# Two layers of graph aggregation and expert blocks: one zero tile for two lists, registers and first tokens at other places, stores on another queue

## The chip, the cores and the metric

The kernel runs on one core of a Trainium2 chip. The metric is the time of one execution on the device in microseconds (us), less is better. Engines are named as in the profile: PE (matrix products and transposes), PEld (its weight loads), DVE (vector), ACT (scalar functions), POOL and SP (issues most DMAs). A trailing q (SPq, PEldq) is the engine's instruction sequencer.

## The reference

The input is x (3327 rows of 256) and a sparse adjacency matrix adj (3327 x 3327). Two layers follow, each an aggregation and a mixture of experts, all on layer-normalized rows and added to x:

```
x = x + relu(adj @ (norm(x) @ W) + b)                             # layer 0, graph
x = x + sum over the top 2 of 8 experts of p_e * FFN_e(norm(x))   # relu, hidden 1024
filt = tanh(adj * adj) * (adj > 0); keep the 700 largest of each row
x = x + relu(filt @ (tanh(norm(x) @ Wp + bp) @ Wg) + bg)          # layer 1, graph
x = x + norm(x) + sum over the top 2 of 8 experts of p_e * FFN_e(norm(x))  # gelu, hidden 256
```

The weights p_e are a softmax over the two largest of eight gate scores.

## The kernel before

Rows are padded to 26 tiles of 128. `x` and the features `s` stay on chip. The adjacency is read twice, as 13 panels of 256 columns, each in two chunks of 1664 KB. A chunk goes into one of the six places of `ring`, called ring_77 to ring_82 in the listings; SP issues the loads (L340), three panels ahead. A panel is 104 products on PE (L358), some 22.5 us.

After each panel `after0` (layer 0) or `after1` (layer 1) works on that panel's two tiles. DVE adds bias and relu (L322, L323), normalizes (L288), forms the gate scores with 16 products (L378), ranks them (L406 to L417), and forms `rt_both`, which expert takes which row. ACT takes the exponential for the softmax (`rt_d`, L443) and DVE finishes the weights (L445 to L447). One panel later `list_tokens` counts rows per expert on PE (`pr`, L464 and L465) and POOL scatters the rows with weight and number (columns WT and ID of a 258-wide row) into a DRAM list, `xlist0` or `xlist1`, in which expert e has NP rows from e*NP (L482).

In layer 0, ACT also counts the non-zeros of every chunk: eight `sign` activations per chunk (L1046, 0.64 us and 0.19 us for reading the sum). ACT works in the order of its queue, so an exponential stands behind the signs listed ahead of it.

The first 256 rows of every expert's part are filled beforehand with zero rows whose ID points to spare output rows. This is `fill`: for each expert it takes a buffer of the pool `blk` (two buffers), clears it on POOL, writes the IDs, and SP stores it (L1013). `fill(xlist0)` is written after panel 0 and `fill(xlist1)` after panel 1; with SP's order, five fills come before panel 3's first load, four behind it, four behind the next, three behind the one after. Ahead of all of them SP issues two transposing copies of the gates, DRAM to DRAM, element by element (L1062).

Once enough tokens are listed, expert blocks of 256 rows ("pairs") run on PE: layer 0 blocks 0 to 29, layer 1 blocks t = 0 to 31 (8 early ones, 18 late pairs, 6 singles of 128 rows). For each block SP loads two table entries into registers (L815, L785), then rows (`xlist`, L820), w1 (L827), b1 (L831), and in layer 0 and for the first blocks of layer 1 also w2 and b2 (L838, L842). PE transposes the rows into `ptb` (L853), DVE (layer 0) or ACT (layer 1) copies that to `xT` (L856), PE forms `ps_h` (L865), ACT applies bias and function (L872, `narrow` in layer 1), PE forms `ps_y` (L904), DVE adds b2 (L911) and scales by the weight (L912), and POOL scatters the result to `ys` (L482). `step` turns the tokens of block t+1 between the two products of block t; block 0's tokens are turned in its own step, after the last panel.

Layer 1 ends in a branch (`inner`, L1297). The usual arm calls `know` first, which loads the expert numbers of the last eight blocks into registers of PE and DVE (L789), and then steps through the late blocks. Between steps it loads finished output rows back (`load_outputs`, ys, L968), adds them to x (`add_loaded`, L982, two additions for each pair of tiles) and stores x to `out` (L1304, on SP). Such a step of pairs is counted by k: k = 0 to 6 are the first 14 tiles, k = 7 to 10 the next 8. The last four tiles come in `finish` after block 31 (L968, L982, and L1266 on ACT's queue).

Of the kernel before, what the change touches and what calls it, by code (L numbers as in the profile page):

```python
# [22 lines left out]
P = 128  # L23
# [67 lines left out]
def gnn_moe_two_layers(  # L91
# [142 lines left out]
    def plain(name, a):  # L234
        t = const.tile(list(a.shape), F32, name=name)
        nc.gpsimd.dma_start(out=t, in_=a)
        return t
# [12 lines left out]
        )  # L250

    g1_bp_sb = plain("g1_bp_sb", g1_bp)
    g1_wg_sb = by_feature("g1_wg_sb", g1_wg)


# [113 lines left out]
    def rows_of(a, t0, n):  # L369
        return a[t0 * P : (t0 + n) * P, :].rearrange("(n p) d -> p n d", p=P)  # L370
# [381 lines left out]
    def experts(xlist, ys, group, fixed, n_hidden, func, w1T, b1, w2T, b2, copy, kept=None):  # L752
# [2 lines left out]

        own_n, all_w2, all_b2 = kept or (EARLY + LATE, None, None)
        pool, several = blk, []
        hc_n = n_hidden // P  # L760

# [15 lines left out]
        def expert(t, late, engines):  # L777

            table, col = late[0] if t >= EARLY else early_table, col_of(t)
            if known and t >= EARLY:  # L780
                if col < known[0]:
                    return col % E
                if engines != [SP]:
                    return known[1][col - known[0]]
            return nc.values_load(table[0:1, 0, col : col + 1], engines=engines, min_val=0, max_val=E - 1)  # L785

        def know(n, late):

            _, registers = nc.values_load_multi_w_load_instructions(  # L789
                late[0][0:1, 0, n : LATE_PAIRS + fixed], engines=[PE, DVE], min_val=0, max_val=E - 1  # L790
            )
            known[:] = [n, registers]

        def col_of(t):
            return t if t < EARLY else order[t - EARLY]
# [9 lines left out]
        def load_one(late):  # L805
            t = len(loaded)
            table = late[0] if t >= EARLY else early_table
            col, n = col_of(t), groups_of(t)
            base = FREE_PAN * NCHUNK + t * places

            def view(name):
                q, at, n = where[name]
                return ring[(base + q) % RING][:, at : at + n]

            row = nc.values_load(  # L815
                table[0:1, 1, col : col + 1], engines=[SP], min_val=0, max_val=E * NP - n * P
            )
            e = expert(t, late, [SP])
            xb = view("xb")[:, 0 : n * RW].rearrange("p (g d) -> p g d", g=n)
            d = nc.sync.dma_start(  # L820
                out=xb, in_=xlist[ds(row, n * P), :].rearrange("(g p) d -> p g d", p=P)
            )
            follow(d, early_rows if t < EARLY else rows_written)
            if t < EARLY:
                tc.add_to_no_dep_group("early" + group, d.ins)
            w1 = view("w1").rearrange("p (c h) -> p c h", c=DC)
            nc.sync.dma_start(  # L827
                out=w1, in_=w1T[ds(e, 1), :, :].rearrange("o (c p) h -> p (o c) h", p=P)
            )
            bb1 = view("b1")  # L830
            d = nc.sync.dma_start(  # L831
                out=bb1, in_=b1[:, ds(e, 1), :].rearrange("p o h -> p (o h)")
            )
            if t >= own_n:
                loaded.append((d, xb, w1, bb1, None, None))
                return
            w2 = view("w2").rearrange("p (c d) -> p c d", d=D)
            nc.sync.dma_start(  # L838
                out=w2, in_=w2T[ds(e, 1), :, :].rearrange("o (c p) d -> p (o c) d", p=P)
            )  # L840
            bb2 = view("b2")
# [76 lines left out]

        ready = {}

        always = EARLY + LATE_PAIRS + fixed

        def step(late, end=always, place=None):
# [23 lines left out]
        def tiers_done():  # L947

            return EARLY + order.index(E - 1) + 1
# [5 lines left out]
        def back_to(old):  # L955
# [5 lines left out]

        return SimpleNamespace(
            load=load, step=step, rest=rest, loaded=loaded, steps_to=steps_to, started=started,
            state=state, back_to=back_to, know=know, tiers_done=tiers_done(), always=always,
        )

    def load_outputs(yt, ys, t0, n, written, group=None):
# [32 lines left out]
    nc.gpsimd.memset(cum[:, 0, :], 0.0)  # L1000
    blk = ctx.enter_context(tc.tile_pool(name="blk", bufs=2))

    def fill(xlist):

        with tc.issue_after(last_feature.ins):
            for e in range(E):
                zeros = blk.tile([P, H // P, SB], F32, name="wide").rearrange("p h b -> p (h b)")
                zeros = zeros[:, 0 : SG * RW].rearrange("p (g d) -> p g d", g=SG)
                nc.gpsimd.memset(zeros, 0.0)
                nc.gpsimd.tensor_scalar(  # L1010
                    zeros[:, :, ID], slot, float(AWAY + SPARE + (LATE + e) * SB), None, ALU.add
                )
                nc.sync.dma_start(  # L1013
                    out=xlist[e * NP : e * NP + SB, :].rearrange("(g p) d -> p g d", p=P),
                    in_=zeros,
                )

# [38 lines left out]
    def after0(pan):  # L1056
        if pan == 0:
            with tc.issue_after(last_piece[0].ins):
                for name, w in (("gate0", f0_wgT), ("gate1", f1_rT)):
                    g = dram.tile([E, D], F32, name=name)  # L1060
                    with nc.allow_non_contiguous_dma("a few thousand elements"):
                        nc.sync.dma_start(out=g.rearrange("e d -> d e"), in_=w)  # L1062
# [151 lines left out]
    def new_layer1():  # L1214
        return experts(
            xlist1, ys1, "1", FIXED[1], D, AF.Gelu, f1_w1, f1_b1, f1_w2, f1_b2,
            nc.scalar.copy, kept=(EARLY // 2, w2_all, gate),
        )

    def after1(layer1, pan):  # L1220
# [11 lines left out]
            for _ in range(NCHUNK):  # L1232
                layer1.load(None)

    def panels1(layer1):
# [32 lines left out]
    with tc.If(first_usual > 0) as arms:  # L1268
# [10 lines left out]
        layer0.steps_to(late, layer0.always)  # L1279
        between()  # L1280
        layer1 = new_layer1()
        aggregate(gnn_b_sb, filter_chunk, panels1(layer1), loaded=ahead)
        late1 = first_blocks(layer1)


# [208 lines left out]
```

## Time and profile before

| | |
|---|---|
| median of three runs | 1244.86 us (1243.46 to 1245.89) |
| profiled execution | 1245.38 us, span 1243.6 us, mean granted clock 0.987 |
| PE busy | 1202.0 us, 97% of the span, 5853 products and transposes |
| panel loads (L340) | 52 of 1664 KB, median 7.3 us to landing |
| fills (L1013) | 16 of 258 KB, median 6.4 us to landing |
| row loads (L820) | 52, median 3.0 us to landing |
| ys loads | 14 of 512 KB, median 5.2 us to landing |

A line of a timeline has the start and the duration in us, the engine, the line of the kernel, the operation, the tile it writes and those it reads, and in brackets how long the engine was idle before it and what ended that. A line of the waits has the engine, what waited, for whom, the total in us, the number of times and the longest. The granted clock is 1.00 at full speed and 0.50 at half.

### The profile page before, as it was taken

The numbers are of one execution on the slowest core, as the hardware profiler recorded it, in microseconds if no ns is written. First come the engines' busy times: TensorE is split into PE (matmuls) and PEld (weight loads), VectorE is DVE, ScalarE is ACT, GpSimd is POOL, SyncE is SP. The second block draws the span as 40 slices with busy tenths as digits, with TensorE's granted clock in tenths as the row PEclk, the third lists the DMA queues.
The fourth block names the chain that finished last, engine by engine and source line by source line (L and its number), as shares of the span: only waits on it lengthen the run. The fifth ranks groups of instructions, "written<-read, shape, count | busy, mean of one in ns | idle before, by whom it ended". The sixth has DMA issues, their size and how long they took to land. (4 is left out here: it accounts for less than half of the span.)

```text
span 1243.6 us, 18251 instructions
## 1 busy us (share of the span) xinstructions
PE 1202.0 (97%) x5853; PEld 1040.3 (84%) x5853; DVE 698.0 (56%) x2812; ACT 522.5 (42%) x963; POOL 280.9 (23%) x367
## 2 busy tenths in 40 slices
PE   7999899999999999999999999999999999999993
PEld 6888788888888888888888888888888888877882
DVE  5064967768755111211111166658999998875464
ACT  4785654551022222222232235895555453043331
POOL 2022313112122111111111110002422323254441
PEclk9999899999999999999999999999999999999997
DMA  9568445544266567575757676344554442476697
GB/s 346 169 194 279 158 169 200 179 146 155 98 215 208 181 197 237 178 230 180 232 173 242 209 273 237 110 149 152 192 182 167 166 176 85 122 247 206 200 296 236
DMA packets 119738, 241.60 MB, mean 194 GB/s; under 512 B 21568, under 2 KB 90192, under 8 KB 112592
## 3 DMA queue, kind: packets, MB, share of 16 engines
q1 hardware_dynamic: 107984, 208.23, 50.2%
q0 software_dynamic: 11104, 31.59, 7.0%
q8 instruction: 48, 0.79, 0.3%
q14 instruction: 58, 0.48, 0.1%
q10 hardware_dynamic: 544, 0.52, 0.1%
HBM read 203.99 MB, written 36.33 MB: 193 GB/s over the span
## 5 line engine op out<-in xcount | busy, mean ns | idle before, releaser
L358 PE MATMUL ps_g<-s,ring 128*128 128x256 f32 x2704 | 591.0, 381 | 0.0
L358 PEld LDWEIGHTS ps_g<-s,ring 128*128 128x128 f32 x2704 | 514.2, 191 | 69.2
L865 PE MATMUL ps_h<-xT,ring 128*128 128x256 f32 (+1 forms) x1176 | 250.1, 366 | 2.7 <-DVE xT L856 1.1
L865 PEld LDWEIGHTS ps_h<-xT,ring 128*128 128x128 f32 x1176 | 205.5, 191 | 39.2 <-ACT wide L872 4.8
L872 ACT ACTIVATE wide<-ps_h,ring 128x256 f32<-128x256 f32 (+1 forms) x240 | 110.2, 459 | 286.0 <-PE ps_h L865 285.0
L378 DVE SCALAR_TENSOR_TENSOR rt_product<-xn,gate 128x256 f32<-128x256 f32 x400 | 197.0, 493 | 12.4
L904 PE MATMUL ps_y<-ring,wide 128*128 128x256 f32 x896 | 200.4, 379 | 0.0
L482 POOL DMA_INDIRECT xlist<-xn,rt_idx x104 | 106.3, 1023 | 371.6 <-DVE ln_ve L269 296.0
L904 PEld LDWEIGHTS ps_y<-ring,wide 128*128 128x128 f32 x896 | 167.2, 190 | 20.9
L1046 ACT ACTIVATE sign<-ring,below 128x416 bf16<-128x416 f32 x208 | 133.5, 642 | 71.6 <-DMA ring<-in_adjT 65.5
L482 POOL DMA_INDIRECT ys<-narrow,index x56 | 54.3, 969 | 331.9 <-DVE narrow L912 245.9
L1197 ACT ACTIVATE ring<-ring 128x3328 f32<-128x3328 f32 x22 | 65.4, 2979 | 87.2 <-DVE ring L1196 56.6
L856 DVE COPY xT<-ptb 128x512 f32<-128x512 f32 (+1 forms) x29 | 19.0, 654 | 146.3 <-PE ptb L853 146.3
L911 DVE TENSOR_TENSOR narrow<-ps_y,ring 128x256 f32<-128x256 f32 x56 | 23.8, 424 | 133.7 <-PE ps_y L904 132.2
L322 DVE TENSOR_TENSOR gnn_t<-ps_g,gnn_b_sb 128x256 f32<-128x256 f32 x52 | 21.9, 421 | 119.4 <-PE ps_g L358 106.4
L482 POOL DMA_INDIRECT ys<-wide,index x58 | 57.8, 996 | 61.2 <-DVE wide L912 35.3
L1198 ACT ACTIVATE ring<-ring 128x3328 f32<-128x3328 f32 x22 | 65.4, 2979 | 0.6
L872 ACT ACTIVATE narrow<-ps_h,ring 128x256 f32<-128x256 f32 (+1 forms) x64 | 28.9, 453 | 68.6 <-PE ps_h L865 66.5
L443 ACT ACTIVATE rt_d<-rt_d 128x2 f32<-128x2 f32 x26 | 5.3, 202 | 123.2 <-DVE rt_d L442 123.2
L904 PE MATMUL ps_y<-s,narrow 128*128 128x256 f32 (+1 forms) x200 | 49.0, 386 | 0.1
L266 DVE BATCH_NORM_STATS2 ln_st<-x 128x6 f32<-128x256 f32 x104 | 42.9, 419 | 6.1 <-DMA x<-in_x 5.0
L1196 DVE TENSOR_SCALAR ring<-ring 128x3328 f32<-128x3328 f32 x22 | 41.3, 1882 | 0.0
(212 smaller groups left out, 983.9 us busy)
## 6 DMA issues: line engine op xcount, KB each, us to landing
ring<-in_adjT SPq DMA_DIRECT2D x52, 1664.0 KB, 7.3
ring<-in_f_w1T SPq DMA_DIRECT2D x30, 1024.0 KB, 6.1
ring<-in_f_w2T SPq DMA_DIRECT2D x30, 1024.0 KB, 7.8
ring<-xlist SPq DMA_DIRECT2D x52, 258.0 KB, 3.0
ring<-in_f_w SPq DMA_DIRECT2D x36, 256.0 KB, 3.6
ring<-ys SPq DMA_DIRECT2D x14, 512.0 KB, 5.2
ring<-in_f_b SPq DMA_DIRECT2D x34, 128.0 KB, 8.0
xlist<-wide SPq DMA_DIRECT2D x16, 258.0 KB, 6.4
```

Of the source, the lines that this page charges most:

```text
L266: nc.vector.bn_stats(out=st, in_=x[:, t0 + g, :])
L358: nc.tensor.matmul(ps[it], lhsT=chunks[k][:, c, ts(it, P)], rhs=s[:, j, :], start=(j == 0), stop=(j == NT - 1),)
L378: nc.vector.scalar_tensor_tensor(product, xn[:, g, 0, 0:D], 1.0, gate[:, e, :], ALU.mult, ALU.mult, accum_out=sc[:, g, e : e + 1],)
L482: d = nc.gpsimd.indirect_dma_start(out=a[:, :], out_offset=bass.IndirectOffsetOnAxis(ap=index, axis=0), in_=rows_, in_offset=None,)
L865: nc.tensor.matmul(ps, lhsT=w1[:, c, ts(hc, P)], rhs=xT[:, c, :], start=(c == 0), stop=(c == DC - 1),)
L872: nc.scalar.activation(hT[:, hc, :], ps, func, bias=bb1[:, hc : hc + 1])
L904: last_product[:] = [nc.tensor.matmul(ps, lhsT=hT[:, hc, ts(g, P)], rhs=w2[:, hc, :], start=(hc == 0), stop=(hc == hc_n - 1),)]
L911: nc.vector.tensor_tensor(y[:, g, :], ps, bb2, ALU.add)
L1046: nc.scalar.activation(sign, a[:, :, ts(i, GROUP)], AF.Sign, bias=below, accum_out=positive[:, pan, i, k : k + 1],)
L1196: nc.vector.tensor_scalar(a, a, 0.0, None, ALU.max)
L1197: nc.scalar.activation(a, a, AF.Square)
L1198: nc.scalar.activation(a, a, AF.Tanh)
```

## The change

`fill` now serves both lists from one tile and is called once, after panel 0. Zeros and row numbers are formed once on POOL. For each list and expert SP issues two DMAs: the zeros of columns 0 to 256, and the numbers into column 257, an element per row. In SP's order all 32 stand ahead of panel 3's first load; the panel loads then follow without fills between them.

The biases b1 of layer 1 are loaded once, early, to `f1_b1_sb`; blocks whose expert is a known number when the code is built (t = 8 to 23) take them from there and have no b1 load.

`turn_first` turns block 0's tokens before the last panel, in both layers; on PE its four transposes stand ahead of that panel's products. In the arms other than the usual one `turn` is not set for layer 1.

`know` only notes the number of known blocks; the registers are loaded by `know_rest` when 22 blocks are started, so on PE the load and its 16 register instructions stand between the second products of one block and the first products of the next. DVE's load keeps its place.

The stores of x to `out` between steps move from SP's queue to ACT's, and the ys loads of the second group (k from 7) come one step later, so that k = 7 to 10 stand behind block 31's loads on SP. On ACT the stores now stand between activations. On DVE the additions of k = 7, 8 and 9 stand ahead of the scaling of blocks 29, 30 and 31; before, those of k = 7 stood ahead of block 30's and the later ones behind block 31's.

```diff
+    f1_b1_sb = plain("f1_b1_sb", f1_b1)
...
-        own_n, all_w2, all_b2 = kept or (EARLY + LATE, None, None)
+        own_n, all_w2, all_b2, all_b1 = kept or (EARLY + LATE, None, None, None)
...
-                if engines != [SP]:
+                if known[1] and engines != [SP]:
                     return known[1][col - known[0]]
...
-        def know(n, late):
-
-            _, registers = nc.values_load_multi_w_load_instructions(
-                late[0][0:1, 0, n : LATE_PAIRS + fixed], engines=[PE, DVE], min_val=0, max_val=E - 1
-            )
-            known[:] = [n, registers]
+        def know(n):
+
+            known[:] = [n, None]
+
+        def know_rest(late):
+
+            _, known[1] = nc.values_load_multi_w_load_instructions(
+                late[0][0:1, 0, known[0] : LATE_PAIRS + fixed], engines=[PE, DVE], min_val=0,
+                max_val=E - 1,
+            )
...
+            if isinstance(e, int):
+                loaded.append((d, xb, w1, all_b1[:, e, :], None, None))
+                return
...
+        def turn_first():
+            ready[0] = turned(loaded[0][1], groups_of(0))
+
...
-    def fill(xlist):
+    def fill(*lists):
+
 
         with tc.issue_after(last_feature.ins):
-            for e in range(E):
-                zeros = blk.tile([P, H // P, SB], F32, name="wide").rearrange("p h b -> p (h b)")
-                zeros = zeros[:, 0 : SG * RW].rearrange("p (g d) -> p g d", g=SG)
-                nc.gpsimd.memset(zeros, 0.0)
-                nc.gpsimd.tensor_scalar(
-                    zeros[:, :, ID], slot, float(AWAY + SPARE + (LATE + e) * SB), None, ALU.add
-                )
-                nc.sync.dma_start(
-                    out=xlist[e * NP : e * NP + SB, :].rearrange("(g p) d -> p g d", p=P),
-                    in_=zeros,
-                )
+            wide = blk.tile([P, H // P, SB], F32, name="wide").rearrange("p h b -> p (h b)")
+            zeros = wide[:, 0 : SG * ID].rearrange("p (g d) -> p g d", g=SG)
+            nc.gpsimd.memset(zeros, 0.0)
...
+            nc.gpsimd.iota(
+                rows_i, pattern=[[SB, E], [P, SG]], base=SPARE + LATE * SB, channel_multiplier=1
+            )
+            nc.gpsimd.tensor_copy(rows_f, rows_i)
+            for xlist in lists:
+                for e in range(E):
+                    first = xlist[e * NP : e * NP + SB, :].rearrange("(g p) d -> p g d", p=P)
+                    nc.sync.dma_start(out=first[:, :, 0:ID], in_=zeros)
+                    with nc.allow_non_contiguous_dma("two elements of a partition"):
+                        nc.sync.dma_start(
+                            out=first[:, :, ID : ID + 1], in_=rows_f[:, e, :].unsqueeze(2)
+                        )
...
-            fill(xlist0)
-        if pan == 1:
-            fill(xlist1)
+            fill(xlist0, xlist1)
...
+        if pan == NPAN - 2:
+            layer0.turn_first()
...
             if pan < NPAN - 1:
                 after1(layer1, pan)
+                if turn and pan == NPAN - 2:
+                    layer1.turn_first()
...
-            layer1.know(2 * E, late1)
+            layer1.know(2 * E)
...
                 for tiles in added:
-                    nc.sync.dma_start(out=rows_of(out, *tiles), in_=x[:, tiles[0] : sum(tiles), :])
+                    nc.scalar.dma_start(out=rows_of(out, *tiles), in_=x[:, tiles[0] : sum(tiles), :])
                 added.clear()
+                if at == EARLY + 2 * E - 2:
+                    layer1.know_rest(late1)
...
-                if waiting and at > waiting[0][1] + 1:
+                if waiting and at > waiting[0][1] + (1 if k < FIRST_TILES // 2 else 2):
...
-            assert not (waiting or asked or added)
+            assert not (waiting or asked)
+            for tiles in added:
+                nc.scalar.dma_start(out=rows_of(out, *tiles), in_=x[:, tiles[0] : sum(tiles), :])
```

More of the change, by code (lines that the diff above doesn't have):

```diff
@@ L826, in load_one @@
             w1 = view("w1").rearrange("p (c h) -> p c h", c=DC)
-            nc.sync.dma_start(
+            d = nc.sync.dma_start(
                 out=w1, in_=w1T[ds(e, 1), :, :].rearrange("o (c p) h -> p (o c) h", p=P)
             )
+            if isinstance(e, int):
+                loaded.append((d, xb, w1, all_b1[:, e, :], None, None))
+                return
             bb1 = view("b1")
@@ L963, in experts @@
             load=load, step=step, rest=rest, loaded=loaded, steps_to=steps_to, started=started,
-            state=state, back_to=back_to, know=know, tiers_done=tiers_done(), always=always,
+            state=state, back_to=back_to, know=know, know_rest=know_rest,
+            turn_first=turn_first, tiers_done=tiers_done(), always=always,
         )
@@ L1001, in gnn_moe_two_layers @@
     blk = ctx.enter_context(tc.tile_pool(name="blk", bufs=2))
-    def fill(xlist):
+    def fill(*lists):
         with tc.issue_after(last_feature.ins):
-            for e in range(E):
-                zeros = blk.tile([P, H // P, SB], F32, name="wide").rearrange("p h b -> p (h b)")
-                zeros = zeros[:, 0 : SG * RW].rearrange("p (g d) -> p g d", g=SG)
-                nc.gpsimd.memset(zeros, 0.0)
-                nc.gpsimd.tensor_scalar(
-                    zeros[:, :, ID], slot, float(AWAY + SPARE + (LATE + e) * SB), None, ALU.add
-                )
-                nc.sync.dma_start(
-                    out=xlist[e * NP : e * NP + SB, :].rearrange("(g p) d -> p g d", p=P),
-                    in_=zeros,
-                )
+            wide = blk.tile([P, H // P, SB], F32, name="wide").rearrange("p h b -> p (h b)")
+            zeros = wide[:, 0 : SG * ID].rearrange("p (g d) -> p g d", g=SG)
+            nc.gpsimd.memset(zeros, 0.0)
+            at = SG * ID
+            rows_i, rows_f = (
+                wide[:, at + i * E * SG : at + (i + 1) * E * SG].rearrange("p (e g) -> p e g", e=E)
+                for i in range(2)
+            )
+            rows_i = rows_i.bitcast(I32)
+            nc.gpsimd.iota(
[10 more added lines that the diff above has]
+                        )
     deviation = {}
@@ L1216, in new_layer1 @@
             xlist1, ys1, "1", FIXED[1], D, AF.Gelu, f1_w1, f1_b1, f1_w2, f1_b2,
-            nc.scalar.copy, kept=(EARLY // 2, w2_all, gate),
+            nc.scalar.copy, kept=(EARLY // 2, w2_all, gate, f1_b1_sb),
         )
@@ L1233, in after1, with panels1 @@
                 layer1.load(None)
-    def panels1(layer1):
+    def panels1(layer1, turn=False):
         def after(pan):
@@ L1281, in gnn_moe_two_layers @@
         layer1 = new_layer1()
-        aggregate(gnn_b_sb, filter_chunk, panels1(layer1), loaded=ahead)
+        aggregate(gnn_b_sb, filter_chunk, panels1(layer1, True), loaded=ahead)
         late1 = first_blocks(layer1)
```

## Prediction

> **What bounds the kernel now.** I read the page's busy table first, then PE's waits, then the timelines of the engines that PE waited for, and last the chain. The page, part 1:
>
> ```profile
> PE 1202.0 (97%) x5853; PEld 1040.3 (84%) x5853; DVE 698.0 (56%) x2812; ACT 522.5 (42%) x963; POOL 280.9 (23%) x367
> ```
>
> PE's waits (what waited, for whom, us in total, times, the longest):
>
> ```profile
> PE ptb L853 <- DMA ring<-xlist: 4.5, 3, 2.4
> PE pr L464 <- DVE rt_both L415: 3.7, 1, 3.7
> PE ps_h L865 <- issue: 2.9, 1, 2.9
> PE ps_h L865 <- DVE xT L856: 1.1, 1, 1.1
> PE ps_h L865 <- ACT xT L856: 0.7, 1, 0.7
> PE ps_h L865 <- DMA ring<-in_f_w: 0.7, 1, 0.7
> ```
>
> PE has matrix work for 97% of the span, and no edit takes any of it away. So what can be won is in PE's few stops, in the half-clock stretches that follow some of them, and in the 17 us after PE's last product. The six waits shown (13.6 us together) are all ones the diff touches. The second is at 134.6. Timelines (start, us, what; in brackets the idle time before it and who ended it), of PE:
>
> ```profile
> 134.03 0.60 PE L358 MATMUL ps_g<-s,ring 128*128 128x256 f32 x2
> 138.34 0.19 PE L464 MATMUL pr<-rt_both,before 128*128 128x8 bf16 x1 [3.72 <-DVE rt_both L415]
> ```
>
> of DVE:
>
> ```profile
> 104.25 0.16 DVE L442 TENSOR_TENSOR rt_d<-rt_v 128x2 f32<-128x2 f32 x1
> 121.62 0.17 DVE L445 TENSOR_SCALAR xn<-rt_d 128x2 f32<-128x2 f32 x1 [17.20 <-ACT rt_d L443]
> ```
>
> and of ACT:
>
> ```profile
> 121.40 0.19 ACT L443 ACTIVATE rt_d<-rt_d 128x2 f32<-128x2 f32 x1
> ```
>
> DVE had panel 1's difference at 104.4, but its exponential stands on ACT behind the eight signs (0.77 us each, 6.15 us) of the second chunk of panel 4, and that chunk came in at 115.3. So DVE stood for 17.2 us, panel 2's routing came 16.7 us after 121.6, and PE stopped for 3.72 us. The windows show what follows: from 137.2 to 144.0 the granted clock is 0.50 with 5.66 us of PE work in it, which is 2.8 us lost. The stop costs 6.5 us in all. The chunk was late because SP, in order, put panel loads between fills that wait for POOL's buffers (SP's timeline):
>
> ```profile
> 18.54 23.69 SPq L1062 DMA_DIRECT2D gate<-in_f_rT  x1
> 42.34 27.74 SPq L1013 DMA_DIRECT2D xlist<-wide  x5
> 70.19 0.41 SPq L340 DMA_DIRECT2D ring<-in_adjT  x1
> 71.72 11.10 SPq L1013 DMA_DIRECT2D xlist<-wide  x4
> 82.92 0.44 SPq L340 DMA_DIRECT2D ring<-in_adjT  x1
> ```
>
> **Part 1, the fill.** Gone from POOL are 15 memsets and 16 additions, beside other work. On SP, 16 fills become 16 zero DMAs (two rows of 257 per partition) and 16 element DMAs (256 pieces of 4 bytes), and all 32 now stand ahead of panel 3's first load instead of 5 fills. Behind them the four loads follow at once. The gates' elements hold this queue until about 60.5 (gate 1: issued at 18.54, 42.3 us to landing). A 258 KB fill keeps the DMA engines for 0.80 us (533 packets from 94 to 96 us, 84% busy, 256 packets a fill). SP's issue is about 0.45 us each, so it does not bind. An element DMA is not in the trace. Its nearest rows are the gates' own 4-byte pieces: 1,972 packets from 39 to 43 us (0.52 us for 256) and 1,950 on that queue from 42 to 52 us (1.31 us). I take 0.9, about halfway. The fill is then through at F = 60.5 + 16 x 1.7 = 87.7; the bounds are 81.6 and 94.3. The first load needs 4 us of engine time (8 packets of 0.5 us on each engine) and about 1.5 us to land: R = F + 5.5 = 93.2.
>
> From there ACT does four chunks without a break: the exponential of panel 1 comes at R + 24.8, panel 2's routing at R + 41.7. PE asks at 134.6, so the delay is R - 92.9 where that is positive, counting a first stop at 112 for panel 1's routing (R + 18) within it. R = 93.2 gives 0.3; the bounds give 0 and 6.9, the latter with up to 2.8 of clock. As the error is one-sided I enter a delay of 1.5: 1.5 - 6.5 = **-5.0** (from -6.5 to +3.2).
>
> The Trainium skill speaks against this edit: "DMA: Bandwidth & Descriptors", section "Rules for kernel authors", says that a DMA whose last dimension is not contiguous becomes one descriptor per element and should be rearranged. The trace agrees on the gates (4-byte packets throughout); it does not say what 256 of them cost from SBUF.
>
> **Part 2, turned tokens.** The four transposes stay on PE (0.63 us in both places) and the copy (0.68 on DVE, 0.58 on ACT) moves under the last panel's 22.5 us. The waits of 1.10 (layer 0) and 0.67 (layer 1) go. The new place adds a wait on block 0's rows: they were asked for at 287.4 and 1058.8 and take 3.0 us (page, part 6), while the panel before the last ends at 322 and near 1072; no stop. **-1.8** (from -1.8 to 0, if the products meet another wait).
>
> **Part 3, registers.** Between the inner branch and the next product, PE's sequencer loads eight registers: 0.61 us, then eight pairs of about 0.3, from 1130.60 to 1133.74, that is 3.14 us. PE stopped for 2.88, and the clock was 0.50 from 1133.86 to 1137.30 (3.44 us, so 1.7 lost): 4.6 in all. The same 3.14 us now stands after block 21. What hides it there is what is queued ahead on PE. Nothing in the trace has a load of this length in the middle of products; where a load of about 0.5 us stands between products (1092.9 to 1098.3) PE stops 0.2 or less, which is one bound, and the other is 2.88 + 1.7 again. I take a lead of 1.2 us (the sequencer at 1138.07 is at a product that starts at 1139.29): 3.14 - 1.2 = 1.9 and no clock loss. **-2.7** (from -4.4 to 0).
>
> The clock is weighed once more: stops of 3.72 and 2.88 were followed by 0.50, one of 2.04 (at 8.1) was not. "TensorE: Matmul & The Clock Gate", Part 1, puts the half clock after an idle window of about 3.4 us on a free-running counter; by that 1.9 would be safe, and 2.88 should have been too, which this trace contradicts.
>
> **Part 4, resident biases.** 16 of the late blocks lose a DMA of SP (0.6 us with its wait). SP is not what PE waits for there; the blocks t = 24 to 31 keep theirs. 0.
>
> **Part 5, the tail.** Here SP is late: an output step takes it 4 to 5 us, a single block 2.25 us of PE. PE's timeline:
>
> ```profile
> 1212.51 0.41 PE L853 MATMUL ptb<-ident,ring 128*128 128x128 f32 x2 [1.06 <-DMA ring<-xlist]
> 1215.79 0.41 PE L853 MATMUL ptb<-ident,ring 128*128 128x128 f32 x2 [1.04 <-DMA ring<-xlist]
> 1221.51 0.44 PE L853 MATMUL ptb<-ident,ring 128*128 128x128 f32 x2 [2.36 <-DMA ring<-xlist]
> 1222.60 2.04 PE L865 MATMUL ps_h<-xT,ring 128*128 128x128 f32 x8 [0.65 <-DMA ring<-in_f_w]
> ```
>
> and the end of the chain that ended last:
>
> ```profile
> 1232.00 5.43 DMA ring<-ys
> 1237.53 0.70 DVE x L982
> ```
>
> The end hangs on block 31's scaling (1227.1): its scatter, the last ys load, the additions, the last store.
>
> With the stores moved to ACT (0.5 us less per step on SP) and the second group of ys loads put after block 31's loads, the loads of blocks 29 to 31 go out near 1204, 1209.5 and 1212.6 (before: 1209.03, 1212.66, 1217.75). The four stops (5.1 us) and the half clock (1.7) go. But two new queues form. On ACT a store waits for its DVE additions, and what is queued behind it are the activations: the stores of the pairs added at 1206.9 and 1211.3 to 1212.7 stand ahead of the activations of blocks 26 and 27, which ran at 1206.6 and 1208.8. Block 27 then starts near 1213, a stop of about 4 us. On DVE the additions of the second group now stand ahead of the scaling of blocks 29, 30 and 31; each waits for a ys load that itself follows a scatter (4.4 us to landing) and takes 5.2 us. Block 26's scatter at 1213.8 gives 1218.2, the load 1223.4, then 1.4 us for each pair of additions, and block 31's scaling comes near 1228.6 to 1229.4 (before 1227.1). The last two loads go out 0.5 instead of 0.97 us apart. So **+1.0**, from -5.5 (both queues are hidden, block 31 scaled at 1221.6) to +4 (a load more in the chain).
>
> **Sum.** Against the profiled execution, 1245.38 (span 1243.6): -5.0 - 1.8 - 2.7 + 0 + 1.0 = -8.5, so 1236.9. The median of before is 0.5 lower than this execution, so 1236.4.
>
> **Rivals.**
> 1. The tail clears: if ys loads land before their additions are asked for, nothing holds block 31 and the tail gives -5.5 instead of +1.0: 1236.4 - 6.5 = 1229.9. For it: four stops do vanish. Against it: scatter and load in series (9.6 us) stand ahead of the scaling. 0.12.
> 2. Slower, by the element DMAs alone: the whole is even with before when they take 1.33 us each, and slower than the bound from 1.5 us (F = 97, R = 102.6: delay 9.7 + 2.8 of clock, against 6.5 + 3.5 won). At 2 us: F = 105.3, R = 110.8, delay 17.9 + 2.8 - 6.5 - 3.5 = +10.7, 1255.6. For it: 4-byte pieces ran at 37 per us from 53 to 57 us, beside the gate's load. Against it: no such load runs after 64 us. 0.15.
> 3. The same near its edge: 1.31 us each, the upper row, gives 1243 to 1245.6. 0.11.
> 4. The register edit does not do what it says: PE stops 2.88 at the new place and loses the clock there too, 1236.4 + 2.7 = 1239.1. 0.07.
>
> My forecast, with its own range of 1232 to 1241, has 0.55. A change of 0.2% (2.5 us) is about what can be told from none. Faster: 0.55 + 0.12 + 0.07 = 0.74. Within: 0.11. Slower: 0.15. The range reaches from the cleared tail to just above rival 3 and leaves out rival 2: 1229 to 1246.
>
> **What would show it.** Right: the wait on rt_both under 2 us, with panel 1's exponential before 119; no wait on xT; none at the branch and about 2 us near block 22; no wait on xlist at the end, but ps_h or ptb waiting for ACT near 1210. Wrong: panel 3's first chunk landing after 100, a stop at 112, or block 31 scaled before 1223.

## The result, and the profile after

Five runs of the changed kernel have a median of 1236.09 us (1233.14 to 1237.78), against 1244.86 (1241.14 to 1247.17, five runs) for the kernel before on the same chip: a ratio of 0.9952 with a 95% interval of 0.9931 to 0.9973. The forecast was 1236.4. The profiled execution took 1235.14 us (span 1233.4). Its page, part 1 (busy us, share of the span, instructions):

```profile
PE 1198.3 (97%) x5853; PEld 1037.4 (84%) x5853; DVE 698.1 (57%) x2812; ACT 522.6 (42%) x963; POOL 271.7 (22%) x339
```

PE has 3.7 us less of work although it does the same products: it ran at half clock for less time. PE's waits (the lines of code have moved by up to 25: `ptb` is now L861, `xT` L864, `ps_h` L873, `narrow` and `wide` L880, the additions L994, the stores L1329, panel loads L341):

```profile
PE ptb L861 <- ACT narrow L880: 5.1, 2, 4.1
...
PE ps_h L873 <- ACT xT L864: 2.1, 1, 2.1
...
PE ps_h L873 <- ACT wide L880: 0.9, 1, 0.9
```

None of the six waits shown of before is left at its place (the one on `xT` from ACT was at layer 1's block 0 and is now at block 22). Three others have come; of the 5.1 us in the first row 1.0 was there before. The timeline of SP shows the last fill and panel 3's first loads, and that of ACT shows panel 1's exponential:

```profile
78.23 0.37 SPq L1037 DMA_DIRECT2D xlist<-wide  x1
79.29 0.83 SPq L341 DMA_DIRECT2D ring<-in_adjT  x2
```

```profile
112.97 0.19 ACT L444 ACTIVATE rt_d<-rt_d 128x2 f32<-128x2 f32 x1
```

The exponential comes at 113.0, where it came at 121.4. The timeline of PE shows the new stops in layer 1's last blocks, the first ahead of block 22, the second between the two products of block 27:

```profile
1176.72 1.69 PE L873 MATMUL ps_h<-xT,ring 128*128 128x256 f32 x5 [2.05 <-ACT xT L864]
...
1201.44 0.69 PE L861 MATMUL ptb<-ident,ring 128*128 128x128 f32 x2 [4.11 <-ACT narrow L880]
```

ACT's timeline shows what held its copy and its activation there: a store of x in its queue (the bracket names DVE, whose addition the store waited for; that addition had waited 1.99 and 3.46 us for its ys load).

```profile
1174.72 0.38 ACTq L1329 DMA_DIRECT2D out_x<-x  x1
1175.19 0.59 ACT L864 COPY xT<-ptb 128x512 f32<-128x512 f32 x1 [2.18 <-DVE wide L919]
...
1200.51 0.40 ACTq L1329 DMA_DIRECT2D out_x<-x  x1
1201.02 0.63 ACT L880 ACTIVATE narrow<-ps_h,ring 128x128 f32<-128x128 f32 x2 [4.98 <-DVE wide L919]
```

At block 27 this is what PE waited for. At block 22 it is not, although the bracket of PE's stop names ACT: the copy was done at 1175.78, and PE started at 1176.72. What ended last there is the load of the registers on PE's own sequencer (its instructions by line: shortest, median and longest in ns, first and last start in us), 0.17 us ahead of the product:

```profile
L794 PEldq SEQ_ASSERT  x8: 18/18/18, 1174.5 to 1176.5; - x8
L794 PEldq TENSOR_LOAD <-s x1: 1036/1036/1036, 1173.2 to 1173.2; - x1
```

The windows (us, PE busy and products, granted clock, DMA share, GB/s) show a stretch at half clock behind each of the two stops:

```profile
1177.50:1181.00 3.50, 3.50 (x12) 0.51 1.00 326
1181.00:1201.40 20.40, 16.26 (x87) 1.00 0.86 265
1201.40:1204.90 3.50, 3.46 (x13) 0.51 0.74 225
```

At the end DVE's timeline has the addition that stands ahead of block 31's scaling (L920), and the chain has the scatter and the last load behind it:

```profile
1215.31 0.69 DVE L994 TENSOR_TENSOR x<-x,ring 128x512 f32<-128x512 f32 x1 [1.05 <-DMA ring<-ys]
1215.92 0.35 DVE L920 TENSOR_SCALAR wide<-wide,ring 128x256 f32<-128x256 f32 x1
```

```profile
1216.55 5.59 DMA ys<-wide,index
...
1223.12 4.50 DMA ring<-ys
```

The same points of PE's work in both traces divide the difference. The last column is the same for one execution of each kernel on a second chip (`r1_before_again` and `r2_after_again` below); all in us, minus is less time than before.

| stage | forecast | profiled pair | second chip |
|---|---|---|---|
| until panel 0's first product (no edit there) | 0 | -3.3 | -2.0 |
| to panel 5 (fill) | -5.0 | -6.7 | -0.6 |
| to the first product of `ps_y` in layer 0 (turn) | -1.1 | -1.4 | -1.4 |
| the blocks of layer 0 | 0 | +1.2 | +1.2 |
| layer 1 to a product in block 15 (turn, registers gone from the branch) | -5.3 | -6.1 | -4.5 |
| from there to PE's end | +2.9 with the next | +3.0 | -0.1 |
| PE's end to the end | | +3.0 | +2.8 |
| sum | -8.5 | -10.2 | -4.5 |

The spans differ by as much (1243.6 to 1233.4, and 1236.7 to 1232.2). The first row has no edit in it, and it differs between executions of one kernel too: panel 0's first product came at 41.0 and 41.8 in two of the changed kernel and at 44.3 and 43.8 in two of the kernel before, but also at 45.5 in another kernel with the same start.

### The profile page after: what moved, and what is told of

Read it like the earlier page. It is cut to its first block, busy times and chain, and to the rows that moved or that the text cites. A ratio compares the mean times of both kernels' runs of the same rounds, so it can differ in the third digit from the quotient of the medians.

```text
span 1233.4 us, 18208 instructions
## 1 busy us (share of the span) xinstructions
PE 1198.3 (97%) x5853; PEld 1037.4 (84%) x5853; DVE 698.1 (57%) x2812; ACT 522.6 (42%) x963; POOL 271.7 (22%) x339
## 5 line engine op out<-in xcount | busy, mean ns | idle before, releaser
L873 PE MATMUL ps_h<-xT,ring 128*128 128x256 f32 (+1 forms) x1176 | 251.1, 366 | 3.3 <-ACT xT L864 2.1
L873 PEld LDWEIGHTS ps_h<-xT,ring 128*128 128x128 f32 x1176 | 205.6, 191 | 40.6 <-ACT wide L880 5.8
L880 ACT ACTIVATE wide<-ps_h,ring 128x256 f32<-128x256 f32 (+1 forms) x240 | 110.3, 460 | 283.9 <-PE ps_h L873 283.0
L864 DVE COPY xT<-ptb 128x512 f32<-128x512 f32 (+1 forms) x29 | 19.0, 654 | 147.0 <-PE ptb L861 147.0
L323 DVE TENSOR_TENSOR gnn_t<-ps_g,gnn_b_sb 128x256 f32<-128x256 f32 x52 | 21.9, 420 | 112.1 <-PE ps_g L359 99.0
L483 POOL DMA_INDIRECT ys<-wide,index x58 | 58.2, 1004 | 60.1 <-DVE wide L920 34.5
L912 PE MATMUL ps_y<-s,narrow 128*128 128x256 f32 (+1 forms) x200 | 49.3, 387 | 0.1
L861 PE MATMUL ptb<-ident,ring 128*128 128x128 f32 x228 | 36.3, 279 | 5.3 <-ACT narrow L880 5.1
```

The lines of the kernel that those rows point to most:

```text
L483: d = nc.gpsimd.indirect_dma_start(out=a[:, :], out_offset=bass.IndirectOffsetOnAxis(ap=index, axis=0), in_=rows_, in_offset=None,)
L861: nc.tensor.transpose(pt[:, c, ts(g, P)], xb[:, g, ts(c, P)], ident)
L873: nc.tensor.matmul(ps, lhsT=w1[:, c, ts(hc, P)], rhs=xT[:, c, :], start=(c == 0), stop=(c == DC - 1),)
L880: nc.scalar.activation(hT[:, hc, :], ps, func, bias=bb1[:, hc : hc + 1])
L912: last_product[:] = [nc.tensor.matmul(ps, lhsT=hT[:, hc, ts(g, P)], rhs=w2[:, hc, :], start=(hc == 0), stop=(hc == hc_n - 1),)]
```

## The experiments

They ran on three chips, on which the kernel before had medians of 1248.84 (25 runs; e1 to e4), 1239.82 (13 runs; r1, r2, e5, e8) and 1249.18 (25 runs; e6, e7, e9, e10). Only ratios of one chip are compared. The changed kernel itself ran on the forecast's chip and on the second, not beside e1 to e4 nor beside e6, e7, e9 and e10; so expectations that are given as a distance from it can't be settled by the times there, only by the stops. The theory was that each term has the cause that the prediction gives it; the rivals were that the stop at 134.6 does not hang on the fill, and that other work sets the new stops.

**The fill alone (`e1_fill_only`).** The kernel before with the new `fill` and nothing else.

```diff
-            fill(xlist0)
-        if pan == 1:
-            fill(xlist1)
+            fill(xlist0, xlist1)
```

> The kernel before with the new fill alone (one tile, 32 DMAs ahead of panel 3's first load). My theory: the wait on rt_both (3.72) and the half clock behind it (2.8) go, nothing else moves: 6.5 us less than before, near 1238.4, first load of panel 3 landing at 88 to 92. Rival: the fill is worth little and the changed kernel's gain lies in its faster start (its first panel began 3.3 us earlier): then within 2 us of before, and rt_both's wait gone or not makes no difference to the end.

Measured: 1246.76, a ratio of 0.9976 (0.9960 to 0.9992), that is 3.0 us less by the ratio (the medians lie 2.1 apart) and not 6.5. No stop on `rt_both`, as expected; the size was missed. The interval, 1.0 to 5.0 us, does not exclude the rival's 2 us.

**The change with the old fill (`e2_old_fill`).** The same edit undone in the changed kernel.

> The changed kernel with the old fill (16 fills between the panel loads). My theory: rt_both's wait of 3 to 4 us and its half clock come back, 6 to 7 us more than the changed kernel: 1242 to 1243. Rival as for the run above: within 2 us of the changed kernel, 1236.

Measured: 1250.19, a ratio of 1.0001 (0.9974 to 1.0028). So all other edits together gave nothing that can be told from none on this chip; the interval leaves 3.3 us either way. But the stop on `rt_both` was not in this profile either: the old fill does not always bring it.

**Both kernels again (`r1_before_again`, `r2_after_again`).**

> The kernel before, unchanged, for a second profile. In the run with the old fill inside the changed kernel there was no wait on rt_both, though the order of SP was the same: the fills there came through 4 us earlier (panel 4's second load issued at 102.3, not 106.5). Theory: the wait of 3.72 is a margin that the old fill sometimes keeps and sometimes not; here panel 4's second load is issued between 102 and 107 and the wait is 3.7 less what it comes earlier, zero at 102.8 or before. Rival: it is always there in the kernel before, since something else than the fill's place differs.

> The changed kernel, unchanged, beside the kernel before on the same chip as the next two. Theory: the first panel load lands well before it is needed in every execution, so no wait on rt_both; 0.4 to 0.8% less than before. The two stops behind stores on ACT (2.05 at block 22, 4.11 at block 27) are there again.

Measured: 1238.52 (one run), and 1236.11 with a ratio of 0.9971 (0.9956 to 0.9986). In this execution of the kernel before, ACT's timeline has panel 1's exponential at

```profile
117.49 0.19 ACT L443 ACTIVATE rt_d<-rt_d 128x2 f32<-128x2 f32 x1
```

and PE stopped for 0.29 us only. SP issued panel 3's first load at 67.5, where the profile of before had 70.19, and the second chunk of panel 4 at 103.2 instead of 106.54. So the kernel before stands near an edge: with the exponential at 117.4 to 117.5 (here and in e2) PE goes on or nearly so, at 121.4 it stops. The other stop of interest was there again, but without a stretch at half clock (PE's timeline, then the windows):

```profile
1127.27 1.96 PE L865 MATMUL ps_h<-xT_arms,ring 128*128 128x256 f32 x8 [2.88 <-issue]
```

```profile
1127.20:1134.00 6.80, 6.73 (x35) 1.00 0.79 242
```

**Each element DMA twice (`e3_elements_twice`).**

```diff
-                        nc.sync.dma_start(
-                            out=first[:, :, ID : ID + 1], in_=rows_f[:, e, :].unsqueeze(2)
-                        )
+                        for _ in range(2):
+                            nc.sync.dma_start(
+                                out=first[:, :, ID : ID + 1], in_=rows_f[:, e, :].unsqueeze(2)
+                            )
```

> The changed kernel with every element DMA issued twice, to measure the price of one and the slack behind them. My theory (0.6 us each, from the changed kernel's trace): the first load of panel 3 lands about 10 us later, near 98.5; panel 2's routing is R + 41.7 = 140, so PE stops for 6 to 9 us in all at the ends of panels 2 and 3, with half clock behind: 7 to 12 us more. Rival (element DMAs ride along beside the zero rows, bounded by SP's issue of 0.45 us): the load lands 7 us later or less and PE stops for under 4 us in all. Second rival (1.3 us each, the upper row of the forecast): 21 us later, stops of 15 us or more.

Measured: 1255.42 (one run). From the first fill to the last took 49.3 us of SP, against 37.0 with single ones: 12.2 / 16 = 0.76 us for each element DMA. The last one stands behind panel 3's first load here; from the first fill to that load it is 47.5 against 38.1 us, 0.63 for each of the 15 more that stand ahead. The exponential and the stop (ACT's timeline, then PE's):

```profile
122.21 0.19 ACT L444 ACTIVATE rt_d<-rt_d 128x2 f32<-128x2 f32 x1
```

```profile
139.12 0.19 PE L465 MATMUL pr<-rt_both,before 128*128 128x8 bf16 x1 [3.07 <-DVE rt_both L416]
```

The stop that the fill removes comes back when its element DMAs take longer, with half clock behind it: from panel 0 to panel 5 PE took 119.2 us, against 112.9 in e1 and e2. One stop of 3.07 came, where the theory had 6 to 9 us in all. This is the mechanism of the prediction's rival 2, made to happen. It also closes the loop: queue, chunk, exponential, stop.

**Without the turned tokens (`e4_no_turn`).** Both calls of `turn_first` left out.

> The changed kernel with block 0's tokens turned in its own step again, in both layers. Forecast's account: two waits of 1.10 and 0.67 come back, 1.8 us more. Theory from the changed kernel's trace: in layer 0 the last panel's exponential (its input ready at 351.9 only) holds ACT anyway, so the stop of 0.94 at block 1 goes when the 1.10 comes back; only layer 1's part is lost: 0.7 to 1.2 us more than the changed kernel, near 1237.

Measured: 1245.43, a ratio of 0.9974 (0.9955 to 0.9993). The stops on `xT` of 1.10 and 0.68 are back. In its place a stop of 0.94 at layer 0's block 1 is gone, which the changed kernel has. ACT's timeline of the changed kernel shows it:

```profile
351.94 0.20 ACT L444 ACTIVATE rt_d<-rt_d 128x2 f32<-128x2 f32 x1 [8.86 <-DVE rt_d L443]
```

The exponential of the last panel stands in ACT's queue ahead of block 1's activations and waits for DVE until 351.9. PE, earlier by the turned tokens, meets it: layer 0 gains 1.4 and gives 1.2 back within two blocks. The time, which is e1's within the noise, tells nothing of the 0.7 to 1.2 us that were expected.

**Stores back on SP (`e5_stores_on_sp`).**

```diff
-                    nc.scalar.dma_start(out=rows_of(out, *tiles), in_=x[:, tiles[0] : sum(tiles), :])
+                    nc.sync.dma_start(out=rows_of(out, *tiles), in_=x[:, tiles[0] : sum(tiles), :])
```

> The changed kernel with the stores between steps back on SP. Theory (a store on ACT waits for its additions with the next block's copies and activations behind it): the 4.11 at block 27 goes; the 2.05 at block 22 falls to the registers' part, about 1.9; SP's loads of the last three blocks are late again and PE waits for rows (before: 1.06, 1.04, 2.36), less with the later ys loads: 1 to 3 us. Whole: within 3 us of the changed kernel, either way. Rival (the stores cost ACT nothing but their 0.4 us): the stops at blocks 22 and 27 stay, and those for rows are added: 3 to 5 us more.

Measured: 1232.56, a ratio of 0.9939 (0.9921 to 0.9956), better than the whole change on the same chip (0.9971; the two intervals touch at 0.9956, the medians lie 3.6 us apart, a little over the 3 that were expected). The stop at block 27 for ACT is gone and SP is late instead (PE's timeline, with block 22's stop ahead):

```profile
1179.26 1.97 PE L873 MATMUL ps_h<-xT,ring 128*128 128x256 f32 x8 [1.62 <-issue]
...
1201.93 0.41 PE L861 MATMUL ptb<-ident,ring 128*128 128x128 f32 x2 [1.50 <-DMA ring<-xlist]
```

ACT's copy was done at 1176.6 here, and PE still stood until 1179.26; its sequencer was at the registers from 1176.1 to 1179.1. The registers alone give block 22's stop.

**Stores given out later in the program (`e8_stores_held`).** Each store is written one step later, in the code's order, on ACT.

```diff
-                for tiles in added:
+                while added and added[0][1] < at - 1 and at <= EARLY + 2 * E:
+                    tiles, _ = added.pop(0)
```

> The changed kernel with its stores still on ACT, but each given out one step later, and those whose turn comes after 24 blocks only when all blocks are started. Theory: no activation stands behind a store that waits; the 4.11 at block 27 and its half clock (1.7) go, the 2.05 at block 22 is left with the registers' part; PE ends 4 to 6 us earlier, and the end gains less, since block 31's scaling still stands behind the additions of k = 9 on DVE: 1 to 4 us less than the changed kernel. Rival (DVE's queue alone sets the end): PE ends earlier, the end moves by less than 0.5 us.

Measured: 1235.97, a ratio of 0.9956 (0.9928 to 0.9985). The edit did not do what it says: in the built program the stores stood between the activations again, and stops of 1.66 (block 22) and 3.54 (1203.5) were there. It tells nothing of the theory.

**The second group one step earlier (`e6_group_step_one`).**

```diff
-                if waiting and at > waiting[0][1] + (1 if k < FIRST_TILES // 2 else 2):
+                if waiting and at > waiting[0][1] + 1:
```

> The change with one edit undone: the second group's ys loads are given out one position after their scatter, as before, not two. Theory (two positions keep the ys loads from standing ahead of block 29 to 31's rows and weights on SP): with one position SP's loads for the last blocks come later again, so PE stops for block rows or weights after 1200 (0.5 to 3 us in all), and the additions come earlier on DVE, so that block 31's scaling moves by less than 2 us either way. Total within 2.5 us of the change. Rival (the position is what makes the additions of the second group stand ahead of block 31's scaling): block 31 is scaled 2 to 3 us earlier, right behind PE's end, and the total is 2 to 3 us less than the change's.

Measured: 1242.20, a ratio of 0.9945 (0.9928 to 0.9962). No stop for block rows or weights came back, against the theory; block 31's scaling was done 2.3 us behind PE's end, in five executions with the change's order (profiled execution, r2, e2, e3, e4) 3.1 to 3.7 us. Its last part, from a product in block 15 to the end, took 79.9 us; in those five it took 83.3, 81.3, 81.9, 81.7 and 80.9. That speaks for the rival, but neither was met in full, and e7, which keeps the two steps, had its scaling done 2.2 us behind PE's end too. So the two steps hold the end up by little, if at all.

**Registers one by one (`e7_registers_by_block`).**

```diff
-                if at == EARLY + 2 * E - 2:
-                    layer1.know_rest(late1)
```

> The change with one edit more: the eight registers of layer 1's last blocks are not loaded in one row behind block 21; PE and DVE load one register each, ahead of the block that uses it. Theory (the row of eight loads is what stops PE at block 22): the stop of 1.7 to 2.1 us at block 22 goes, no single register load stops PE by more than 0.4 us, and the total is 1 to 2 us less than the change's where no half clock follows the stop, 3 to 4 where one does. Rival (the activations held up by a store on ACT set block 22's start, and the registers only end beside them): a stop of 1 to 2 us stays at block 22, put down to ACT, and the total is the change's within 1 us.

Measured: 1247.52, a ratio of 0.9990 (0.9975 to 1.0005). A stop of 1.50 stays at block 22, put down to ACT, as the rival had it. ACT's timeline:

```profile
1187.47 0.38 ACTq L1329 DMA_DIRECT2D out_x<-x  x1
1187.94 0.59 ACT L864 COPY xT<-ptb 128x512 f32<-128x512 f32 x1 [2.51 <-DVE wide L919]
```

Here the copy is done at 1188.53 and PE starts at 1188.58. With e5 this is a table of four: the row of registers alone gives 1.62, the store on ACT alone 1.50, both 1.63 to 2.05, neither none (e10; e9 ties the store behind the arithmetic). Where both are there, the registers end last in every profile, and PE starts 0.17 to 0.20 us behind them. The two lie beside each other, so that taking one away wins next to nothing. And the single loads are not free. They stop PE in seven of the last eight blocks, ahead of the second product (PE's timeline, three of them):

```profile
1204.91 1.99 PE L912 MATMUL ps_y<-s,narrow 128*128 x8 [0.49 <-DVE index L894]
...
1208.81 1.13 PE L912 MATMUL ps_y<-s,narrow 128*128 x4 [0.51 <-issue]
...
1212.76 1.13 PE L912 MATMUL ps_y<-s,narrow 128*128 x4 [0.66 <-issue]
```

The seven (0.33 to 0.66) add up to 3.1 us, more than the row behind block 21 costs.

**Stores on SP and registers one by one (`e10_sp_registers`).** e5's and e7's edits together.

> The change with the stores on SP again, and the eight registers loaded one by one. Theory: as with the stores on SP alone (ratio to the kernel before 0.9939 on another chip, where PE's stop at block 22 was 1.62 us, by the registers), less that stop: 1 to 1.6 us less, a ratio of 0.992 to 0.993. Rival (SP is the next in line): PE, earlier by 1.6 us, waits 1 to 1.6 us longer for block rows on SP near the end, and the ratio stays 0.994.

Measured: 1244.30, a ratio of 0.9958 (0.9945 to 0.9972), a miss: no stop at block 22, but 0.22 to 0.92 in seven of the last eight blocks, 3.4 us together. The rival missed as well, as none of them is for block rows. From the product in block 15 to the end it took 79.7 us, against 79.1 in e5: what the one stop gave, the others took.

**A version from the findings (`e9_best`).** Stores stay on ACT, but each is tied to the last activation given out before it; those of the last rows, and the second group's additions, come behind the last activation and block 31's scaling; registers one by one.

```diff
+                    with behind(last_h):
+                        nc.scalar.dma_start(out=rows_of(out, *tiles), in_=x[:, tiles[0] : sum(tiles), :])
...
+            for yt, tiles, _ in asked:
+                with behind(last_y):
+                    add_loaded(yt, *tiles)
```

> A version made from the findings: stores stay on ACT, but each stands behind the activations of the block in progress when it is given out; the stores of the last rows stand behind all activations; the additions of the second group stand behind block 31's scaling; registers are loaded one by one. Theory (stores that wait for DVE on ACT's queue, the row of register loads, and the additions ahead of the last scaling are what the change leaves): no stop over 1 us for ACT or registers from block 22 on, so PE ends 4 to 7 us earlier than with the change; block 31 is scaled right behind PE; the chain behind it (scatter, load, additions, store) is as long or up to 1.5 us longer, as more additions and stores stand behind it. Total 3 to 6 us less than the change. Rival (SP's rows and weights are next in line): 2 to 4 us of stops for block rows or weights come in their place and the total is 0 to 2 us less.

Measured: 1241.51, a ratio of 0.9942 (0.9921 to 0.9962). From block 22 on the longest stop is 0.37 us. On DVE's timeline the scaling of block 31 comes right behind the last product (PE ended at 1219.21), with the additions behind it:

```profile
1219.71 0.35 DVE L920 TENSOR_SCALAR wide<-wide,ring 128x256 f32<-128x256 f32 x1
1219.98 1.29 DVE L994 TENSOR_TENSOR x<-x,ring 128x512 f32<-128x512 f32 x2
```

From the product in block 15 to the end it takes 77.1 us, the least of all: with the change 80.9 to 83.3, before 77.3 and 78.6, e5 79.1. So the change's end is 2 to 6 us longer than before's, and that can be had back, but not at the place that was expected. Up to PE's end it takes 57.7 us here (with the change 60.1 to 63.0); from there to the end 19.4 remain, against 17.3 and 17.0 before and 19.2 to 21.9 with the change, although block 31 is scaled right behind PE. In e5 it is scaled as early, and 20.4 us remain. So the late scaling is not what keeps this last part long in these two; the chain there runs through ys loads of 4.7 to 6.7 us (e9) and 6.2 and 7.7 (e5), and no run takes them apart. As the change itself did not run on this chip, the gain over it rests on these stretches; by medians, e9 and e6 can't be told apart.

## Why the prediction was right, and where it was not

The direction and the time were right on the chip of the forecast. On the second chip the change was worth 0.29%, 3.7 us by the medians where 8.5 had been forecast; on the chip of e1 and e2 the fill alone gave 0.24% and all else together nothing that can be told from none. The terms one by one:

- **Fill, -5.0.** The chain was right (queue, chunk, exponential, stop), and e3 made it run backwards. Panel 3's first load was issued at 79.3 and its chunk was there at 88.5, the exponential 24.5 us later: forecast R = 93.2 and R + 24.8. It was 4.7 us early because four of the 16 pairs of a zero and an element DMA were issued before 60.5, where the sum lets the fill begin, and the other twelve took 1.38 us each, not 1.7, with the DMA engines 98% busy from 62 to 79 us. The element DMA took 0.63 to 0.76 (e3), inside the bounds of 0.52 and 1.31 and below the 0.9 taken. The rule of the Trainium skill that was weighed there ("DMA: Bandwidth & Descriptors", section "Rules for kernel authors": one descriptor per element) names a real cost, 10 to 12 us of SP's queue in all; here the loads ahead had room for it, and in e3, with twice as much, they had not. The step that failed is the 6.5 us that is taken away: stop and clock of one execution, entered as if all had them. In r1 only 0.29 us of stop was there and no half clock, and in runs side by side, on another chip, the fill was worth 3.0 us (1.0 to 5.0 by e1's interval).
- **Turned tokens, -1.8.** Both waits went (e4 brings them back). Layer 0's 1.4 is given back to a wait that the prediction allowed for only in the bound ("if the products meet another wait"): the exponential of the last panel, in order on ACT.
- **Registers, -2.7.** The branch gave its 2.88, with 1.7 of clock in the profiled pair and none in r1. The new place stopped PE for 1.62 (e5, alone) against 1.9. In the profiled execution it was 2.05, as the load ahead of the eight steps took 1.04 us there (0.60 and 0.61 in e5 and r2), and then the half clock followed, which the term denied: 3.75 us against 1.9, nearer to rival 4's 4.6. In r2 it was 1.66 without half clock. Left out was that the store on ACT holds `xT` at the same block; with the registers there it costs nothing more, without them 1.50 (e7).
- **Biases, 0.** PE waits on no bias in any profile. ACT waits for one up to 1.3 us, in blocks that keep their load, and DVE up to 2.8 us in layer 0; no stop of PE is put down to either.
- **Tail, +1.0.** The queues were the ones named: the four stops for SP went, block 27 waited 4.11 for a store on ACT (forecast about 4), and the additions stood ahead of block 31's scaling. Mis-sized were the clock behind that stop (1.7, not counted) and the new chain: the scaling came at 1215.9, 2.8 us behind PE's last product (before 0.5), and then its scatter took 5.59 to landing (before 3.45). Counted from the product in block 15, it came 5.4 us later than before, 2.3 on the second chip, where 1.5 to 2.3 had been forecast. From that product on the pair lost 6.0 us, where the tail and the new stop at block 22 were put at 2.9.

By the letter one sign of being wrong was met: block 31 was scaled before 1223. The sign is written in times of the kernel before, and the changed kernel was 16.2 us ahead of these by block 15, so it tells nothing.

In the profiled pair the tail and layer 0 came out 4.3 us worse than forecast, and the start, 3.3 us earlier without an edit, and a fill stage 1.7 us better made up for it. On the second chip the fill's stage gave 0.6. That the median came within 0.3 us of the forecast is therefore luck in part. Of the rivals, the cleared tail did not come (e9 needed three more edits for a shorter one), and slow element DMAs did not either. Rival 3's price does not come out of its terms: the fill's bound of 1.31 us puts +0.4 to +3.2 in the place of -5.0, which gives 1241.8 to 1244.6, not 1243 to 1245.6.

## What to carry to other kernels

A stop that one profile shows may be a margin that some executions miss: profile the kernel twice before a removed stop is entered at its full length. A DMA that waits on an engine's in-order queue holds that engine's arithmetic for as long (here PE stood 4.11 us for it); tie it behind the arithmetic, or leave it on the queue of an engine that does none. Where two edits move work to the same place, look for what they hold together, since taking away either alone may give nothing; and where a view puts a stop down to one engine, look when that engine was done.

## What the runs showed of the hardware

**The clock is decided in fixed windows.** In all 14 profiled executions the granted clock changed (from 20 us on) only at multiples of 3.413 us from one another. Counting PE's idle time in each such window, worked out from the records: up to PE's last product all 21 windows with 2.02 us or more were followed by one at half clock; between 1.5 and 2.02, 4 of 14; below 1.5, only four, which were at half clock themselves. So what counts is how much of a stop falls in one window. The 2.05 us at block 22 lay in one and cost 1.7 us more. The 2.88 us of r1 fell on two, 1.44 and 1.45, and cost nothing more. The Trainium skill, "TensorE: Matmul & The Clock Gate", Part 1, gives such a free-running window of 3413 ns, and the runs agree; it puts the half clock after a whole idle window, and here about 2 us of one were enough.

**A slow stretch on two of the chips.** In every profile of e1 to e4, e6, e7, e9 and e10 PE stopped several times in the first blocks of layer 1 (1104 to 1139), for up to 3.7 us, with half clock at least once; in none of the others did it stop there for more than 1.0 except at the branch. From layer 1's first product of `ps_y` to the first one of block 14 those of them with the change took 64.1 to 69.7 us, and such kernels on the other two chips 57.5 to 57.6: 6.5 to 12.3 us more, where the medians of the kernel before lie 4.0 to 9.4 apart. In e7 DVE's short instructions, singly or in pairs, came 0.7 us apart there, whatever their length (in the profiled execution of the change the same three are 0.26 and 0.42 apart):

```profile
1107.01 0.35 DVE L550 TENSOR_REDUCE pl_end<-pl_ee 128x24 f32<-128x192 f32 x1 [0.24 <-issue]
1107.71 0.18 DVE L597 TENSOR_TENSOR pl_v<-pl_v,pl_baset 128x23 f32<-128x23 f32 x1 [0.35 <-DVE pl_end L550]
...
1108.43 0.23 DVE L552 TENSOR_SCALAR pl_end<-pl_end 128x8 f32<-128x8 f32 x1 [0.21 <-issue]
```

What slows it was not found, and no run tells it apart.
